# A mixture of experts that starts on the rows routed so far, while the last rows are still being routed

## The chip, the cores and the metric

The kernel runs on one core of a Trainium2 chip. A core has five engines that run side by side, each through its own instructions in order: TensorE (PE, matrix products; PEld is its loading of weights), VectorE (DVE), ScalarE (ACT), GpSimd (POOL) and SyncE (SP, which mostly issues DMAs). They wait for each other through semaphores. The metric is the device time of one execution in microseconds, and lower is better.

## The reference

A graph network of four layers over 2708 nodes with 256 features. Each layer is a graph part and a feed-forward part. The feed-forward part of the third layer (`_L2_ffn_ref`) is what the change touches: causal attention with four heads, and then a mixture of eight experts, of which each row uses its two best.

```python
x = x + y @ wo.T                                   # attention's result, added to the rows
flat = _rmsnorm(x, ln2_w).reshape(-1, Cx)
probs = jax.nn.softmax(flat @ router_w.T, axis=-1) # 8 experts
tp, ti = jax.lax.top_k(probs, TOPK)                # the best 2
tp = tp / (jnp.sum(tp, axis=-1, keepdims=True) + 1e-09)
weights = jnp.sum(tp[..., None] * jax.nn.one_hot(ti, NE, dtype=flat.dtype), axis=1)
for e in range(NE):
    hh = jax.nn.silu(flat @ w1[e].T) * (flat @ w3[e].T)
    out = out + weights[:, e:e + 1] * (hh @ w2[e].T)
return x + out.reshape(Bx, Tx, Cx)
```

Here `Bx*Tx` is the 2708 nodes. The experts' inner width is 682. The fourth layer's graph part (called g3 in the kernel) follows, and needs `W` and `a` of its own.

## The kernel before

**Attention** (`attention`) goes over the queries in six blocks: five of 512 columns and one of 148. Within a block, `attend` walks over the key tiles of 128 rows up to the diagonal. For each tile TensorE makes the scores (`sc`), ACT the exponential (`e`), DVE masks the diagonal, TensorE adds to the numerator (`po`), and the exponentials are summed for the denominator. These sums are kept in two parts: every third tile is added by GpSimd, the others by DVE. At the end of the block TensorE sums each part over its rows (`pd`), DVE takes the reciprocal and multiplies. The last block has both pairs of heads in one pass (m == 2) over 22 key tiles, the other blocks take one pair at a time.

**Routing** runs beside it. `send(n)` is a generator for the rows of one block: it multiplies with `wo` (`wy`), adds the result to `X`, normalises the row (`h`), makes the router's logits (`pr`), takes the first and second maximum, ranks the rows of each expert (`rank`), and scatters every row to two places of the DRAM tensor `hs` with indirect DMAs on GpSimd. In `hs` each expert has room for all rows, filled from the front. `between` moves the waiting generators on after each key tile, by a share of `steps[1]`. The rows of block n are sent during block n + 1. Those of the last block have no block after them: `send` for them runs alone, and then `finish` counts the rows of the experts and works out which expert each of 47 slot tiles of 128 rows belongs to. Slots 0 to 7 are always the first 128 rows of experts 0 to 7.

**The mixture** (`experts`) goes over the slot tiles with the function `through`. Per tile s: `fetch` loads the rows `f` from `hs` (on SP), `front` transposes them (`tp`, then a copy `ft` on ACT), `hidden` makes the two inner products `h0` (with `w1`) and `h1` (with `w3`), `silu` and `gate` combine them on ACT and DVE into `hh`, `transposes` transposes that on TensorE (`pt`) and copies it out (`ht`, partly on DVE and partly on ACT), `results` multiplies with `w2` (`po`), ACT copies to `y`, and GpSimd scatters `y` to the DRAM tensor `ys`. `place` (`where`) works out on DVE where these rows go in `ys`: to the node's row, or to a spare row where the slot is empty. It needs `own`, `taken` and `spare`, which `owners` makes after `finish`. In between stand `shares` (the softmax over the experts and the weights of the two choices) and, called from it, `Head`, which loads g3's `W` and `a` (`g3w`, `av`) through GpSimd's DMA queue and folds them on DVE. Tiles past the 47 are under a branch (`others`), for the case that the rows fall on the experts so unevenly that 47 don't suffice. The expert weights of one kind are 5.5 MB: `w1` comes in when the projections' room comes free, `w3` when attention's does.

The order of instructions on each engine is set at build time. `tc.issue_after` holds what stands under it behind a given instruction. Pools of buffers are opened and closed in the program's text, and what is opened in a closed pool's room waits for that room's last readers.

The lines touched: `decoder_ffn` (L1333), `Routing.finish` (L1528), `others` (L1596), `load` (L1613), `where` (L1633), `attention` (L1691) with `attend` and `send`, and `experts` (L1951).

Of the kernel before, what the change touches and what calls it, by code (L numbers as in the profile page):

```python
# [8 lines left out]
F32 = mybir.dt.float32  # L9
# [1323 lines left out]
def decoder_ffn(net, ctx):  # L1333

    nc, tc, a = net.nc, net.tc, net.a
    big = ctx.enter_context(tc.tile_pool(name="d_big", bufs=1))
    dram = ctx.enter_context(tc.tile_pool(name="d_dram", bufs=1, space=bass.MemoryType.DRAM))
    route = Routing(net, big, dram, 2, "d")  # L1340
    ln2 = net.load_rows(big, a["d_ln2"], D, "ln2")
    router = net.load_weight(big, a["d_routerT"], "router")
    with ExitStack() as inner:
        weights = Weights(net, inner)
        attention(net, route, ln2, router, weights)
        route.finish()
        prep = ctx.enter_context(tc.tile_pool(name="g3prep", bufs=1))
        work = inner.enter_context(tc.tile_pool(name="d_wt", bufs=1))
        heads = []

        def shares():

            route.weights(work)
            total = work.tile([P, NT], F32, name="total")
            nc.vector.tensor_tensor(total, route.weight[:, 0, :], route.weight[:, 1, :], ALU.add)
            nc.vector.tensor_scalar(total, total, 1e-9, None, ALU.add)
            nc.vector.reciprocal(total, total)
            for c in range(2):
                nc.vector.tensor_tensor(route.weight[:, c, :], route.weight[:, c, :], total, ALU.mult)
            heads.append(Head(net, prep, work, "g3", False))  # L1360

        experts(net, route, weights, shares)
    return heads[0], route
# [32 lines left out]
class Routing:  # L1396

# [6 lines left out]
    def __init__(self, net, pool, dram, choices, key):  # L1404
# [59 lines left out]
        nc.vector.memset(self.local[:, :E], 0.0)  # L1464
        self.total = pool.tile([P, E], F32, name=f"{key}total")
# [62 lines left out]
    def finish(self):  # L1528
# [4 lines left out]
        with tc.tile_pool(name=f"{self.key}finp", bufs=1, space=PSUM) as psum:  # L1533
            ps = psum.tile([P, E], F32, name="total")
            nc.tensor.matmul(ps, net.ones, self.count, start=True, stop=True)
            nc.vector.tensor_scalar(n, ps, 1.0, -1.0, ALU.max, ALU.add)
            nc.vector.tensor_copy(total, ps)
# [19 lines left out]
        nc.vector.tensor_copy(self.further, sums[:1, 3, 4 + E - 1 :])  # L1557

# [36 lines left out]
    @contextmanager  # L1595
    def others(self):  # L1596

        more = self.net.nc.values_load(self.further, min_val=0, max_val=self.tiles)
        with self.net.tc.If(more > self.usual - self.E):
            yield  # L1600
# [12 lines left out]
    def load(self, s, f):  # L1613

        sync = self.net.nc.sync
        if s < self.E:
            self.loaded = sync.dma_start(f, self.hs[s * CAP : s * CAP + P, :])
            return

        with nullcontext() if s == self.usual else self.net.tc.issue_after(self.loaded.ins):  # L1620
            row = sync.value_load(
                self.row[0:1, s : s + 1], min_val=0, max_val=(self.E - 1) * CAP + (NT - 1) * P
            )
        rows_of = self.hs[bass.ds(row, P), :]
        self.loaded = sync.dma_start(f, rows_of.rearrange("p d -> d p") if self.choices == 1 else rows_of)
# [7 lines left out]
    def where(self, work, s, f):  # L1633

        nc = self.net.nc
        to = work.tile([P, 1], I32, name="to", bufs=8)
        at = work.tile([P, 1], F32, name="second", bufs=3)
        nc.vector.tensor_scalar(  # L1638
            at, f[:, D + 1 :], self.own[:, s : s + 1], float(NT * P), ALU.not_equal, ALU.mult
        )  # L1640
        nc.vector.tensor_scalar(at, at, f[:, D : D + 1], self.taken[:, s : s + 1], ALU.add, ALU.mult)
        nc.vector.tensor_tensor(to, at, self.spare[:, s : s + 1], ALU.add)
        return to

    def send(self, to, y):
# [10 lines left out]
        tc.add_to_no_dep_group(f"{self.key}results", i.ins)  # L1656
        return i
# [33 lines left out]
def attention(net, route, ln2, router, weights):  # L1691
# [11 lines left out]
    with ExitStack() as ctx:  # L1703
        rp = ctx.enter_context(tc.tile_pool(name="a_r", bufs=2))
        one = ctx.enter_context(tc.tile_pool(name="a_one", bufs=1))
        psc = ctx.enter_context(tc.tile_pool(name="a_sc", bufs=2, space=PSUM))
        pso = ctx.enter_context(tc.tile_pool(name="a_o", bufs=2, space=PSUM))
        aux = ctx.enter_context(tc.tile_pool(name="a_x", bufs=2, space=PSUM))
# [12 lines left out]
        core = ctx.enter_context(ExitStack())  # L1721
# [71 lines left out]
        def attend(n, p):  # L1793
# [3 lines left out]
            if p == 0:  # L1797
                results[n] = rp.tile([P, 2, 512], F32, name="yt")
# [13 lines left out]
            for j in range(last + 1):  # L1812
# [7 lines left out]
                part = j % 3 == 2  # L1820
# [9 lines left out]
                nc.scalar.activation(ev, by_heads(ps[:r])[:, :, :, o:], AF.Exp, scale=DH**-0.5)  # L1830
# [22 lines left out]
            nc.vector.tensor_tensor(y, y, by_pairs(po), ALU.mult)  # L1853

        def send(n):
# [6 lines left out]
            for k, t in enumerate(its):  # L1862
                r = rows(t)
                po = aux.tile([P, D], F32, name="wy", tag="aux")
                net.matmul_k(po[:r], yt[:, :, k * P : k * P + r], wo)
                xa = xs[t] = rp.tile([P, D], F32, name="xa", bufs=4)
# [3 lines left out]
                h = hs[t] = rp.tile([P, D + 2], F32, name="h", bufs=8)  # L1870
# [9 lines left out]
            for k in range(0, len(its), 2):  # L1880
                pair = its[k : k + 2]
                ps = aux.tile([P, 2, 2 * P], F32, name="tp", tag="aux")
# [10 lines left out]
                pr = aux.tile([P, 2, 8], F32, name="pr", tag="aux")  # L1893
# [12 lines left out]
            yield from route.chunk(rp, aux, its[0], len(its), hs.__getitem__, tag="aux")  # L1906
# [18 lines left out]
        for n in range(len(cols)):  # L1925
# [4 lines left out]
            if n:  # L1930
                waiting.append(send(n - 1))
                steps[1] += 14
            for p in range(len(queries[n])):
                attend(n, p)
# [3 lines left out]
            waiting.clear()  # L1938
        core.close()
        weights.more()  # L1940
        for _ in send(len(cols) - 1):
            pass
# [8 lines left out]
def experts(net, route, weights, shares):  # L1951
# [4 lines left out]
    with ExitStack() as ctx:  # L1956
# [7 lines left out]
        def fetch(s):  # L1964
            fs[s] = work.tile([P, D + 2], F32, name="f", bufs=5)
            route.load(s, fs[s])
# [7 lines left out]
        def place(s):  # L1974
            tos[s] = route.where(work, s, fs.pop(s))
# [23 lines left out]
        def silu(s):  # L1999
# [3 lines left out]
            nc.scalar.activation(h2, halves.pop((s, 0))[:, :, :HALF], AF.Silu)  # L2003

        def gate(s):
            h2 = hhs[s][:, :HID].rearrange("p (q m) -> p q m", q=2)
            nc.vector.tensor_tensor(h2, h2, halves.pop((s, 1))[:, :, :HALF], ALU.mult)

        def transposes(s):
# [5 lines left out]
            nc.vector.tensor_copy(ht[:KP, :4, :], pt[:KP, 0])  # L2015
# [14 lines left out]
        def through(s0, s1):  # L2030


            for s in range(s0, min(s0 + 4, s1)):
                fetch(s)
# [5 lines left out]
            silu(s0)  # L2040
            front(s0 + 1)
# [3 lines left out]
            if s0 == 0:  # L2045
                route.owners()
            place(s0)
            place(s0 + 1)
            if s0 == 0:
                shares()  # L2050
            for s in range(s0, s1):
# [8 lines left out]
                silu(s + 1)  # L2060
                with tc.issue_after(last.ins):
                    last = results(s, ht)
                if s + 4 < s1:
                    fetch(s + 4)
                if s + 2 < s1:
                    with tc.issue_after(last.ins):
                        front(s + 2)
                        place(s + 2)
# [6 lines left out]
                gate(s + 1)  # L2075

        through(0, route.usual)
        with route.others():
            through(route.usual, route.tiles)
# [191 lines left out]
```

## Time and profile before

| | |
|---|---|
| time, median of 3 runs | 2853.9 us (2853.67 to 2859.36) |
| time of the profiled execution | 2853.26 us |
| its span | 2851.6 us |
| PE, DVE, ACT, POOL busy | 92%, 51%, 36%, 13% of the span |
| last attention block: first `po` to last `po` | 2056.05 to 2103.3 us |
| first transposes of the mixture | 2134.51 us |
| last `y` copied, last scatter issued | 2535.84, 2536.48 us |

The span is what the profiler saw from the first to the last instruction; the device time is about 1.7 us more. All places in time below are microseconds from the span's start. Busy time of TensorE is no measure of its speed, since matrix products overlap and the clock granted to it can be less than full; so the text goes by the waits and by the stretch concerned.

### The profile page before, as it was taken

How to read it: one execution, taken by the hardware profiler on the slowest of the kernel's cores; microseconds unless marked ns; L12 is line 12 of the kernel's file. 1: busy time of each engine (PE TensorE's matmuls, PEld its weight loads, DVE VectorE, ACT ScalarE, POOL GpSimd, SP SyncE). 2: the span in 40 equal slices, each digit the busy share in tenths (PEclk: the TensorE clock that was granted, in tenths of full speed). 3: DMA queues.
4: the chain of work that ended last, by engine and by line, in shares of the span. 5: the costliest groups of instructions: out<-in, count | busy, mean ns of one | idle time of the engine just before them, and what ended most of it. 6: DMA issues, size and time to landing. Idle time of an engine off the chain costs nothing.

```text
span 2851.6 us, 32365 instructions
## 1 busy us (share of the span) xinstructions
PE 2625.3 (92%) x11712; PEld 1616.6 (57%) x11712; DVE 1446.4 (51%) x3086; ACT 1040.0 (36%) x1639; POOL 381.5 (13%) x470
## 2 busy tenths in 40 slices
PE   5999989799999999888999899999969999969998
PEld 4667746563333444577788533333337777757885
DVE  7753348453777765422544456464653222245555
ACT  3344433224665653311543223233322221225453
POOL 1000012100000001143300123223331111110002
PEclk9999999797999999989999999899979999989999
DMA  8899210000000003753200100002031111041001
GB/s 295 288 299 326 97 65 1 3 5 1 1 1 1 1 3 115 169 176 128 85 1 1 34 23 18 16 0 94 16 117 32 30 30 34 28 137 62 1 1 40
DMA packets 107336, 197.67 MB, mean 69 GB/s; under 512 B 8831, under 2 KB 64361, under 8 KB 104341
## 3 DMA queue, kind: packets, MB, share of 16 engines
q1 hardware_dynamic: 89178, 147.89, 16.4%
q0 software_dynamic: 14624, 43.22, 4.6%
q10 hardware_dynamic: 3374, 4.46, 0.5%
q8 instruction: 98, 1.61, 0.2%
q14 instruction: 62, 0.50, 0.1%
HBM read 135.82 MB, written 59.71 MB: 69 GB/s over the span
## 4 chain that ended last, share of the span: by engine, by line
PE 74%; DVE 9%; issue 5%; DMA 5%; ACT 3%; POOL 3%; another core or an unknown queue 0%; ACTq 0%; SPq 0%; POOLq 0%; DVEq 0%
PE acc L1310 15%; PE acc L805 8%; PE acc L284 7%; PE den L816 4%; PE po L2022 4%; PE po L1836 3%; PE sc L1817 3%; PE score L273 3%; PE pv L123 3%; PE h L1990 3%; DMA f<-hs 2%; PE h L943 2%; PE po L123 2%; PE sc L1785 2%; PE pl L123 1%
## 5 line engine op out<-in xcount | busy, mean ns | idle before, releaser
L675 DVE SCALAR_TENSOR_TENSOR e<-e,mask 128x768 f32<-128x768 f32 (+2 forms) x264 | 411.3, 1573 | 310.2 <-ACT e L674 309.9
L674 ACT ACTIVATE e<-big_p,minus_one,ratio 128x768 f32<-128x768 f32 (+2 forms) x264 | 394.9, 1513 | 368.4 <-PE acc L1310 229.7
L1310 PE MATMUL acc<-V,e 128*128 128x257 f32 (+1 forms) x1936 | 433.5, 383 | 4.5 <-DVE e L675 4.4
L1310 PEld LDWEIGHTS acc<-V,e 128*128 128x128 f32 (+1 forms) x1936 | 352.3, 186 | 85.7 <-issue 32.1
L805 PE MATMUL acc<-e,V 128*64 128x512 f32 (+1 forms) x1056 | 244.3, 551 | 4.4 <-DVE e L675 4.4
L1990 PE MATMUL h<-w,ft 128*128 (+1 forms) x752 | 233.5, 453 | 0.5 <-ACT ft L1972 0.5
L284 PE MATMUL acc<-F,e 128*128 128x257 f32 x968 | 226.3, 384 | 3.1 <-DVE e L281 2.7
L284 PEld LDWEIGHTS acc<-F,e 128*128 128x128 f32 x968 | 173.4, 185 | 67.1 <-DVE e L281 28.5
L805 PEld LDWEIGHTS acc<-e,V 128*64 128x64 f32 x1056 | 107.5, 137 | 163.8 <-issue 131.2
L1817 PE MATMUL sc<-qt,kt 64*128 64x512 f32 (+5 forms) x568 | 177.2, 576 | 4.1 <-ACT e L1830 2.4
L1830 ACT ACTIVATE e<-sc 128x1024 f32<-128x1024 f32 (+3 forms) x120 | 99.6, 859 | 188.8 <-PE sc L1817 169.4
L1990 PEld LDWEIGHTS h<-w,ft 128*128 128x128 f32 x752 | 136.1, 191 | 56.7 <-issue 1.4
L281 DVE TENSOR_TENSOR e<-e,mask 128x512 f32<-128x512 f32 (+2 forms) x132 | 80.4, 625 | 150.3 <-ACT e L275 148.7
L1842 DVE TENSOR_TENSOR sum<-sum,e 128x1024 f32<-128x1024 f32 (+4 forms) x88 | 100.1, 1138 | 77.2 <-ACT e L1830 70.0
L275 ACT ACTIVATE e<-score 128x512 f32<-128x512 f32 (+2 forms) x132 | 69.7, 544 | 179.1 <-PE score L273 152.5
L2022 PE MATMUL po<-w,ht 114*128 (+1 forms) x564 | 129.5, 379 | 0.9 <-DVE ht L2015 0.9
L1836 PE MATMUL po<-e,V 128*64 128x512 f32 (+3 forms) x480 | 111.7, 547 | 16.8 <-ACT e L1830 8.7
L816 PE MATMUL den<-e,low 128*3 128x512 f32 (+1 forms) x1056 | 123.8, 542 | 0.3 <-DVE e L675 0.3
L2022 PEld LDWEIGHTS po<-w,ht 114*128 114x128 f32 x564 | 106.7, 189 | 22.6 <-DVE ht L2015 8.2
L1638 DVE TENSOR_SCALAR second<-f,down 128x1 f32<-128x1 f32 x47 | 9.9, 213 | 213.2 <-DMA f<-hs 213.2
L1817 PEld LDWEIGHTS sc<-qt,kt 64*128 64x128 f32 (+1 forms) x568 | 60.8, 191 | 94.1 <-issue 78.0
L273 PE MATMUL score<-QK 128*128 128x512 f32 (+2 forms) x264 | 112.1, 555 | 1.2 <-ACT e L275 0.7
(618 smaller groups left out, 3510.9 us busy)
## 6 DMA issues: line engine op xcount, KB each, us to landing
row<-in_adj SPq DMA_DIRECT2D x21, 1354.0 KB
raw<-in_adjT SPq DMA_DIRECT2D x35, 768.0 KB
hs<-zero SPq DMA_DIRECT2D x8, 2838.0 KB
hidden<-hr SPq DMA_DIRECT2D x34, 256.0 KB
wd<-in_f_wd SPq DMA_DIRECT2D x8, 1024.0 KB
kept<-mask SPq DMA_DIRECT2D x21, 338.5 KB
mask<-kept SPq DMA_DIRECT2D x21, 338.5 KB
f<-hs SPq DMA_DIRECT2D x47, 129.0 KB
```

What stands on the lines that cost most here:

```text
L123: self.nc.tensor.matmul(out, lhsT[:, c, :], rhs[:, c, :], start=first and c == 0, stop=last and c == n - 1)
L273: nc.tensor.matmul(ps[:r, :iw], QK[:, 0, span(j)], QK[:, 1, i0 : i0 + iw], start=True, stop=True)
L284: nc.tensor.matmul(acc[k][:ri], e[:r, k * P : k * P + ri], F[:r, j, :], start=j == 0, stop=j == NT - 1)
L674: nc.scalar.activation(v, big_p[:, i], AF.Relu, bias=net.minus_one, scale=ratio)
L675: return nc.vector.scalar_tensor_tensor(v, v, 1.0, net.mask[:, j, i], ALU.add, ALU.mult)
L805: made = nc.tensor.matmul(acc[n][half, :iw], V[:, j, h, :], e[:, k, i0 : i0 + iw], start=j == 0, stop=j == NT - 1)
L816: made = nc.tensor.matmul(den[g : g + Q, :iw], low[:, j, h, Q - 1 - q : 2 * Q - 1 - q], e[:, k, i0 : i0 + iw], start=False, stop=j == NT - ...
L1310: nc.tensor.matmul(acc[k][:ri], e[:, k * P : k * P + ri], V[:, j, :], start=j == 0, stop=j == NT - 1)
L1817: nc.tensor.matmul(by_pairs(ps[:r, g])[:, :, o:], kt[b, span(j)], qt[b, :, o:iw], start=True, stop=True)
L1836: nc.tensor.matmul(by_pairs(po[b])[:, :, o:], V[:r, j, g, :], by_pairs(e[:r, g])[:, :, o:], start=j == 0, stop=j == last,)
L1990: last = nc.tensor.matmul(halves[s, n][:, q, :HALF], fts[s][:, c, :], weights.w13[n][:, es[s], c, q * HALF : (q + 1) * HALF], start=c == 0 ...
L2022: last = nc.tensor.matmul(po, ht[:KP, k, :], w2[:KP, es[s], k, :], start=k == 0, stop=k == KC - 1)
```

## The change

Attention now ends by calling the mixture, with a generator for the rest of the routing, and the mixture runs that generator beside its first tiles.

- The rows of the fifth block are sent faster during the sixth: the count of steps for the last block is 24 instead of 14.
- In the last block all exponentials are summed on DVE, in one part; the result has a tile of its own, `yl`.
- `cut` counts the rows that each expert has had from the first five blocks (`so_many`), and makes `own`, `taken` and `spare` for slots 0 to 7 from that count.
- The first eight tiles are fetched at once, three on ACT's queue and five on GpSimd's, without waiting for the last block's rows, and are placed by the cut's counts. A row of the last block that would have come into one of these tiles is missing from it: `finish` counts these, and if there is any, the branch `others` runs all eight again.
- ACT loads Silu's table ahead of the first tile (`warm`).
- `routing()` is what runs beside the tiles: `send` of the last block, then `finish`, `owners` and `Head`, each one or more `step()`s. A step stands behind the last product of its place in the tile's work. `finish`, `owners` and `Head` are also held behind a given `ht` copy on DVE, and placing is held behind a gate.
- The tiles of the routing in PSUM share the one buffer of the mixture's `tp`.
- `shares` is taken apart from `Head` and stands at the end of the 47 tiles.

```diff
 def decoder_ffn(net, ctx):
+    prep = ctx.enter_context(tc.tile_pool(name="g3prep", bufs=1))
     with ExitStack() as inner:
         weights = Weights(net, inner)
-        attention(net, route, ln2, router, weights)
-        route.finish()
...
+        def head(work):
             heads.append(Head(net, prep, work, "g3", False))
 
-        experts(net, route, weights, shares)
+        def mixture(after, rest):
+            experts(net, route, weights, after, rest, head, shares)
+
+        attention(net, route, ln2, router, weights, mixture)
```

```diff
 class Routing:
+    def cut(self, psum, tag):
+        nc, E, pool, key = self.net.nc, self.E, self.pool, self.key
+        ps = psum.tile([P, E], F32, name="so_many", tag=tag)
+        nc.tensor.matmul(ps, self.net.ones, self.count, start=True, stop=True)
+        self.had = pool.tile([P, E], F32, name=f"{key}had")
+        nc.vector.tensor_scalar(self.had, ps, float(P), None, ALU.min)
+        own, taken, spare = self.cuts = [pool.tile([P, E], F32, name=f"{key}cut{k}") for k in range(3)]
+        nc.vector.tensor_scalar(own, self.part, self.at, None, ALU.add)
+        nc.vector.tensor_scalar(taken, self.had, self.at, None, ALU.is_gt)
+        nc.vector.tensor_tensor(spare, taken, self.place[:, :E], ALU.mult)
+        nc.vector.tensor_tensor(spare, self.place[:, :E], spare, ALU.subtract)
...
     def finish(self, psum=None, tag="total"):
...
+        if self.cuts:
+            missing = self.pool.tile([1, 1 + E], F32, name=f"{self.key}missing")
+            nc.vector.tensor_scalar(missing[:, 1:], total[:1], float(P), None, ALU.min)
+            nc.vector.tensor_tensor(missing[:, 1:], missing[:, 1:], self.had[:1], ALU.subtract)
+            nc.vector.tensor_reduce(missing[:, :1], missing[:, 1:], AX.X, ALU.add)
+            nc.vector.scalar_tensor_tensor(
+                self.further, missing[:, :1], float(S), sums[:1, 3, 4 + E - 1 :], ALU.mult, ALU.add
+            )
...
     def load(self, s, f, engine=None):
...
-            self.loaded = sync.dma_start(f, self.hs[s * CAP : s * CAP + P, :])
+            self.loaded = (engine or sync).dma_start(f, self.hs[s * CAP : s * CAP + P, :])
...
-    def where(self, work, s, f):
+    def where(self, work, s, f, cut=False):
+        own, taken, spare = self.cuts if cut else (self.own, self.taken, self.spare)
```

```diff
 def attention(...)
         def attend(n, p):
-                part = j % 3 == 2
+                part = j % 3 == 2 and m == 1
...
-        def send(n):
+        def send(n, rp, aux, tag="aux"):
...
-                steps[1] += 14
+                steps[1] += 14 if n + 1 < len(cols) else 24
...
+        route.cut(aux, "aux")
         core.close()
         weights.more()
-        for _ in send(len(cols) - 1):
-            pass
+        mixture(exp, lambda *work: send(len(cols) - 1, *work))
```

```diff
 def experts(...)
-        def through(s0, s1):
-            for s in range(s0, min(s0 + 4, s1)):
-                fetch(s)
+        def through(s0, s1, beside=iter(()), cut=False):
+            def step():
+                with tc.issue_after(last.ins):
+                    next(beside, None)
+
+            for s in range(s0, min(s0 + (E if cut else 4), s1)):
+                fetch(s, (nc.scalar if s < 3 else nc.gpsimd) if cut else None)
...
             silu(s0)
+            step()
             front(s0 + 1)
             for q in range(2):
                 last = hidden(s0, 1, q)
             gate(s0)
-            if s0 == 0:
-                route.owners()
-            place(s0)
-            place(s0 + 1)
-            if s0 == 0:
-                shares()
+            step()
+            with tc.issue_after(gates[-1].ins):
+                place(s0, cut)
+                place(s0 + 1, cut)
             for s in range(s0, s1):
...
                 silu(s + 1)
+                step()
                 with tc.issue_after(last.ins):
                     last = results(s, ht)
-                if s + 4 < s1:
+                step()
+                if s == 4:
+                    for _ in beside:
+                        pass
+                if s + 4 < s1 and (s + 4 >= E or not cut):
                     fetch(s + 4)
...
                 gate(s + 1)
+                step()
+                if s + 2 < s1:
+                    with tc.issue_after(gates[-1].ins):
+                        place(s + 2, cut and s + 2 < E)
...
+        def routing():
+            pool = ctx.enter_context(ExitStack())
+            yield from rest(pool.enter_context(tc.tile_pool(name="e_r", bufs=1)), pf, "tp")
+
+            with tc.issue_after(copied[-1].ins):
+                route.finish(pf, "tp")
+            yield
+            yield
+            with tc.issue_after(copied[-1].ins):
+                route.owners()
+            yield
+            pool.close()
+            room = ctx.enter_context(tc.tile_pool(name="e_room", bufs=1))
+
+            with tc.issue_after(copied[-1].ins), tc.issue_after(route.sent.ins):
+                head(room)
+            rooms.append(room)
+
+        with tc.issue_after(after.ins):
+            nc.scalar.activation(work.tile([P, 1], F32, name="warm", bufs=1), net.ln_eps, AF.Silu)
+        through(0, route.usual, routing(), True)
+
+        with tc.issue_after(silus[-1].ins), tc.issue_after(gates[-1].ins):
+            shares(rooms[0])
         with route.others():
+            through(0, E)
             through(route.usual, route.tiles)
```

Here `after` is the last exponential of attention, `copied`, `gates` and `silus` are lists of the instructions put out so far, and `route.sent` is the last scatter of a tile's result.

## The prediction

> **What bounds the kernel now.** I read the page first (span 2851.6 us, PE busy 92%), then the chain of waits in the stretch that the change touches, then TensorE's timeline there, then the windows for the granted clock. The mixture (`experts`, 47 tiles) is TensorE work end to end: from 2149.88 us every tile is the same chain.
>
> ```profile
> 2107.83 1.28 PE pd L1848 x4
> ...
> 2133.73 4.60 DMA av<-in_g_a
> ...
> 2149.88 3.44 PE h L1990 x12
> 2153.32 0.75 PE pt L2014 x6
> 2154.07 1.15 PE h L1990 x4
> 2155.22 2.59 PE po L2022 x12
> 2157.81 0.22 PE tp L116 x2
> ```
>
> Columns are start, duration, what. A tile costs 3.44+0.75+1.15+2.59+0.22 = 8.15 us of TensorE and nothing else. Ahead of that lies a hole. TensorE's timeline (brackets: idle before, and who ended it):
>
> ```profile
> 2107.83 1.25 PE L1848 MATMUL pd<-sum,ones 128*64 128x296 f32 x4 [3.77 <-POOL sum L1842]
> 2111.68 3.90 PE L123 MATMUL wy<-wo,yt 128*128 128x256 f32 x8 [2.60 <-DVE yt L1853]
> ...
> 2134.51 0.66 PE L116 MATMUL tp<-ident,f 128*128 128x128 f32 x2 [9.30 <-POOL hh L2001]
> 2135.64 4.78 PE L1990 MATMUL h<-w,ft 128*128 128x341 f32 x8 [0.46 <-ACT ft L1972]
> ```
>
> Attention's last `po` ends at 2103.34. Then TensorE waits for GpSimd's partial sum, for DVE's reciprocal, and for the routing of the last two row tiles, until the first mixture tile starts at 2134.5. From 2103.34 to the second gate's matmuls at 2149.88 are 46.5 us, for 11.7 us of mixture work at full speed.
>
> ```profile
> 2105.00:2106.00 1.00, 0.00 (x0) 0.00 (x0) 0.00 (x0) 0.00 (x0) 0.69 (x2) 1.00 0.37 132
> 2106.00:2107.00 1.00, 0.00 (x0) 0.00 (x0) 0.00 (x0) 0.00 (x0) 0.97 (x2) 0.51 0.16 58
> ...
> 2139.00:2140.00 1.00, 1.00 (x3) 0.56 (x2) 1.00 (x5) 0.00 (x0) 0.00 (x0) 0.50 0.00 0
> 2140.00:2141.00 1.00, 1.00 (x5) 0.61 (x5) 1.00 (x6) 0.55 (x1) 0.00 (x0) 0.92 0.00 0
> ```
>
> The third number from the end is the granted clock: it falls to a half about 2.0 us after TensorE stops (2104.0), and is back 5.6 us after it works again (2134.5). A stall costs twice.
>
> ```profile
> 2132.37 17.86 SPq L1617 DMA_DIRECT2D f<-hs  x8
> ...
> 2135.60 1.28 ACT L2003 ACT_TABLE_LOAD   x1
> ```
>
> The first rows `f` were read by TensorE 2.1 us after their issue; a table load on ACT takes 1.28 us.
>
> [...] the trace shows 1.28 and an ACTIVATE straight behind it at 2538.43, so I take 1.28.
>
> **The change, step by step.** Times are on the profiled run's axis (run 2853.26, span 2851.6; the median shown is 2853.9, so sums carry over within 0.6 us).
>
> S1, last attention block. The third of the sums that GpSimd did (7 adds of 1.45 us) goes to DVE (0.78 each, 5.5 us in all); `send` of the block before is squeezed from all 22 key tiles into about the first 13 (24 steps instead of 14). DVE was busy about 29 of 50 us there. In the squeezed part I count reciprocal and product 4.0, adds 10.1, `send` 15.7 = 29.8 us of DVE against 36 us of TensorE, so DVE is tight but not the bound: 0 to 3 us lost, I take 1. Gain: the scatters of that block end by about 2099 instead of 2111.5, and `pd` no longer queues behind GpSimd's scatters. With one more add (0.8) `pd` ends at 2104.4, not 2109.08.
>
> S2, first rows. ACT loads Silu's table once the last `po` and the scatters are done: 2103.4+1.28 = 2104.75, then issues three `f` loads (0.43 each on SP); +2.1 = 2106.85. The `w3` load (8 x 682 KB) starts at the same moment, because it still waits for `pd`. From nothing to 2 us on top; I take 0.75: 2107.6. `w3`'s first expert is needed only about 2114, and 682 KB at the 400 GB/s of windows 2114 to 2126 take 1.7 us, so it hides. The other five `f` go through GpSimd (about 0.8 us an issue), needed tiles later.
>
> S3, first tile. TensorE has stood for 3 us, so half clock: transposes 0.66, copy 0.46, 8 x 0.57 = 4.6, to 2113.3. Full clock after that: `wy` of 128 rows 0.86, `h` with `w3` 2.3, next transposes 0.22, `wy` of 20 rows 0.86: 2117.6. Then `h` 2.3, `pt` 0.75, `po` 2.59, `tp` 0.22 and 0.5 for an `ht` copy that stands behind two placings and the start of the inverse root on DVE: 2124.0. This is the place that was 2149.88. **Gain 25.9.** DVE's reciprocal (2.0) and product (0.46) now lie beside `f`'s latency.
>
> S4, routing beside tiles 1 to 3. TensorE still does it: transposes 0.5, `pr` 1.06, `rank` 0.8, `total` 0.4 = 2.8 us, now at full clock. **Loss 2.8.** On DVE the first-max chain (about 5 us) fits between an `ht` copy (0.69) and the gate (0.87) of a tile. `finish` does not quite: `rank`'s followers 2 us, then about 14 ops of 0.2 and 3 of 0.47 before gate 3. That gate comes about 1.8 us late, and the `ht` copy behind it, with one 0.47 reduce and five small ops between, 0.7 more. **Loss 2.3** (0 to 5). `owners` (3.4 us) fits in the next tile.
>
> S5, `Head` (g3's folded weights). Its two DMAs are issued on GpSimd behind the scatter of tile 3, and DVE reaches its first op behind gate 4 and a placing. Tile 3's `po` ends about 2153.35; y copy 0.4, scatter 1.3, `g3w` 0.8, so `av` is issued at 2155.9. Landing: 4.7 us in this trace (2133.73 to 2138.43, beside eight `f` loads), 2.9 for the similar load at 572.0 (DVE read it at 574.9). I take 3.0: 2158.9. Eight ops, about 3.0, then the `ht` copy 0.69: 2162.6. TensorE wants that copy after `h` and `pt` of the next tile, 2158.95. **Loss 3.7** (0 to 6), and TensorE has stood long enough for half clock: 3.7 us at half cost 1.9. **Loss 1.9** (0 to 2.8). Queued behind DVE's wait are this copy, ACT's copy of the other chunks, `po` 4, and through it everything.
>
> S6, things without price. `hs` scatters of the last block stand on GpSimd before tile 2's `y` scatter (4 x 1.28): three `y` buffers give it two tiles, 16 us. The SP load of tile 8 waits for these scatters and `row`, ready about 2155, needed near 2180. `shares` moves to the end: 15 DVE ops, about 4 us, and an Exp with a table load; the weight is first used at 2545.29, 9 us after the last `y` copy (2535.84), and three of the ops stand before the last `ht` copy in what was a 0.96 us idle. At most 0.1; without that cover about 4. The branch for experts short at the cut never runs: in the reference, the first 2560 rows give each expert at least 485.
>
> Sum: 25.9 - 2.8 - 2.3 - 3.7 - 1.9 - 1 (S1) = **14.2 us**: 2853.26 - 14.2 = **2839**.
>
> **Rivals.**
> A, better: `av` lands early or the clock stays up, so S5 costs little and S4 hides: gain 18 to 24, 2829 to 2835. For: first-tile work is all dependency-free by then. Against: in this trace DVE waited for `av` both times a `Head` was built (12.6 us in three waits with the first graph's).
> B, worse: DVE is the bound in the last block (S1's 3) and in tiles 1 to 4 (S4 5, S5 6+2.8) and `f` comes 2 us later: 25.9-2-2.8-5-8.8-3 = gain 4, 2844 to 2851. For: DVE's order is fixed, so one late input holds gates and copies. Against: DVE was busy 25.6 of 40 us even in the hole.
> C, slower: the half clock stays. Bursts at 2107.83 (1.25 us) and 2111.68 (3.9 us) left it at 0.50. If gaps of over 2 us recur in tiles 0 to 4, their 41 us of TensorE work run at half: 41 us more, of which my sum holds 4.7 and the stalls 6 lie inside: gain 14 turns into a loss of 10 or more, about 2864. It decides once the half clock lasts 30 us longer than I count. Against: my gaps are one at the start and one in tile 4, with about 50 us between.
>
> **Numbers.** Forecast case (gain 9 to 18, 2835 to 2844) 0.60; A 0.17; B 0.15; C 0.07; nothing measurable 0.01. Half of B's upper end lies within 0.2% (5.7 us, what a measurement of this kernel can tell). Faster 0.87, same 0.06, slower 0.07. The range takes the forecast case, most of A and most of B: 2831 to 2848.
>
> **What would show it.** S1 and S2: `pd` near 2104, `f` read near 2107. S3: the second gate's first matmul near 2124. S4: a gate some 2 us late in tile 3. S5: DVE waiting for `av` with `po` of tile 4 some 4 us late, and one dip of the clock. S6: first use of the weight unchanged after the last `y`. It is wrong if `f` comes after 2111, if DVE runs behind from the last block on, or if the clock stays at a half past tile 0.

## The result

The changed kernel took **2825.6 us** (median of 4 runs, 2823.7 to 2828.0) beside 2854.3 for the kernel before (4 runs, 2853.7 to 2859.4): ratio 0.9891, 95% interval 0.9876 to 0.9906. That is 28.7 us less, twice the 14.2 that I forecast, and outside my range. The profiled execution took 2823.73 us, its span is 2822.0.

A line of the page of the changed kernel:

```profile
L2046 DVE TENSOR_TENSOR hh<-hh,h 128x682 f32<-128x682 f32 x47 | 40.7, 865 | 247.5 <-PE h L2029 247.5
```

This is DVE's gate (busy us and mean ns, then idle us before it and what ended that): DVE's idle time in the mixture (247.5 us) now ends with TensorE's products. The page before has no such row among its costliest; that idle time stood in another row:

```profile
L1638 DVE TENSOR_SCALAR second<-f,down 128x1 f32<-128x1 f32 x47 | 9.9, 213 | 213.2 <-DMA f<-hs 213.2
```

There DVE waited 213.2 us for the loads of the tiles' rows. The gate itself needs TensorE's products and no load: where DVE stood waiting for a load, something else stood in front of the gate in its queue.

TensorE around the start of the mixture, changed kernel (start, duration, what, in brackets idle before and who ended it):

```profile
2103.60 0.72 PE L1870 MATMUL po<-e,V 128*64 128x296 f32 x4 [1.46 <-DVE e L1868]
...
2107.22 0.66 PE L116 MATMUL tp<-ident,f 128*128 128x128 f32 x2 [1.43 <-DMA f<-hs]
2108.39 4.60 PE L2029 MATMUL h<-w,ft 128*128 128x341 f32 x8 [0.52 <-ACT ft L2011]
...
2123.24 2.17 PE L2029 MATMUL h<-w,ft 128*128 128x341 f32 x7
```

The first transposes come at 2107.22 where they came at 2134.51, and the second gate's first product at 2123.24 where I forecast 2124.0. So the part that I worked out at length looks right to 0.8 us. That is partly luck: counted from the last attention block's first result `po`, which came 3.1 us later in this execution (below), the place is 3.9 us earlier than forecast. Where is the rest? The gates, one for each of the 47 tiles, mark the mixture's pace, so I cut the span at the first results of the last attention block (its first `po`), at gates 0, 7 and 46, and at the end. Microseconds, from the start times of these instructions in the profiles:

| kernel | first `po` to gate 0 | to gate 7 | to gate 46 | to the end | sum |
|---|---|---|---|---|---|
| before | 88.1 | 57.4 | 328.8 | 321.3 | 795.6 |
| changed | 57.3 | 67.1 | 317.9 | 320.5 | 762.9 |
| difference | -30.8 | +9.8 | -10.9 | -0.8 | -32.7 |

The changed kernel's profiled execution reached the first `po` 3.1 us later (2059.14, not 2056.05). In other executions below this place lies anywhere from 2049.1 to 2059.7, though no edit touches what lies before it; I don't count it. The last column but one also moves by 3 us among kernels that are the same there.

So the first two stretches gained 21.0 us together, and **10.9 us came in 39 tiles of the steady mixture**, which my sum didn't touch. In the kernel before, the gates came 8.15 us apart up to the seventh, then 8.49 us (34 intervals, 2193.06 to 2481.65), then 8.15 again for the last ones. In the changed kernel they are 8.155 apart from gate 5 to gate 45. The chain of waits of the kernel before says why, in a stretch that I hadn't looked at:

```profile
2198.84 2.00 DMA f<-hs
...
2200.87 0.23 DVE second L1638
...
2201.51 0.88 DVE hh L2007
...
2207.04 0.23 PE tp L116 x2
...
2207.29 2.07 DMA f<-hs
```

The products `h` that the gate reads are not what it waits for. The chain goes: transposes `tp` of a tile, then the load of rows `f`, then DVE's three placing operations (`second`, `second`, `to`), then the gate `hh`, then TensorE. A placing of some tile stands before the gate in DVE's queue, its rows are loaded only when `tp` has freed a buffer, and the gate waits behind. The same DVE stretch in the changed kernel:

```profile
2305.94 0.87 DVE L2046 TENSOR_TENSOR hh<-hh,h 128x682 f32<-128x682 f32 x1 [5.64 <-PE h L2029]
2306.72 0.21 DVE L1668 TENSOR_SCALAR second<-f,down 128x1 f32<-128x1 f32 x1
```

Here the gate comes first and waits for TensorE alone, and the placing follows.

In the source both kernels place tile s+2 at about gate s+1. But the source order isn't the order of DVE's queue. In the built kernel before, nothing ties the placing to the gate, and the scheduler moved it up as far as the buffers let it: ahead of gate k the queue holds the placing of tile k+**6**. With five `f` buffers, the rows of tile k+6 go into the buffer of tile k+1, and TensorE transposes that one just before gate k. And what stands ahead of the gate there holds it, as the traces show: in the changed kernel a gate starts 2.79 us after the transposes before it (2303.15 and 2305.94), here 3.08 us after (2198.43 and 2201.51), right behind `to`, which started at 2201.43. The gate stood about 0.3 us behind work that it doesn't need. Up to the seventh gate only the first of the three operations stood ahead of it and the gate was not late; from the eighth on, all three did.

### The profile page after: what moved, and what is told of

It is laid out like the page before. It is cut to its first block, busy times and chain, and to the rows that moved or that the text cites. A ratio compares the mean times of both kernels' runs of the same rounds, so it can differ in the third digit from the quotient of the medians.

```text
span 2822.0 us, 32381 instructions
## 1 busy us (share of the span) xinstructions
PE 2612.0 (93%) x11710; PEld 1613.5 (57%) x11710; DVE 1451.8 (51%) x3102; ACT 1041.2 (37%) x1641; POOL 375.3 (13%) x469
## 4 chain that ended last, share of the span: by engine, by line
PE 77%; DVE 7%; issue 5%; DMA 4%; ACT 3%; POOL 2%; SPq 0%; ACTq 0%; POOLq 0%; DVEq 0%
PE acc L1310 15%; PE acc L805 8%; PE acc L284 7%; PE h L2029 7%; PE den L816 4%; PE po L2061 4%; PE po L1870 4%; PE sc L1850 3%; PE score L273 3%; PE pv L123 3%; PE h L943 2%; PE sc L1816 2%; PE po L123 2%; DMA dys<-y,to 2%; PE pl L123 1%
## 5 line engine op out<-in xcount | busy, mean ns | idle before, releaser
L1864 ACT ACTIVATE e<-sc 128x1024 f32<-128x1024 f32 (+4 forms) x121 | 100.2, 857 | 186.4 <-PE sc L1850 170.1
L2046 DVE TENSOR_TENSOR hh<-hh,h 128x682 f32<-128x682 f32 x47 | 40.7, 865 | 247.5 <-PE h L2029 247.5
L1876 DVE TENSOR_TENSOR sum<-sum,e 128x1024 f32<-128x1024 f32 (+5 forms) x95 | 104.7, 1102 | 77.4 <-ACT e L1864 74.2
L1870 PE MATMUL po<-e,V 128*64 128x512 f32 (+4 forms) x484 | 113.2, 546 | 17.2 <-DVE e L1868 9.0
```

The source lines that it names most:

```text
L1870: nc.tensor.matmul(by_pairs(po[b])[:, :, o:], V[:r, j, g, :], by_pairs(e[:r, g])[:, :, o:], start=j == 0, stop=j == last,)
```

## The experiments

Three theories of the 10.9 us. **1, order:** the placing ahead of the gate costs it, and the change's hold (`issue_after(gates[-1].ins)`) took it away. **2, late rows:** five `f` buffers are too few, and the change's eight cured it. **3:** the gain comes from the end of the mixture or the last graph layer. The first two experiments change the kernel before, the others the changed one.

### Only the hold, in the kernel before

```diff
                     with tc.issue_after(last.ins):
                         front(s + 2)
-                        place(s + 2)
...
                 gate(s + 1)
+                if s + 2 < s1:
+                    with tc.issue_after(gates[-1].ins):
+                        place(s + 2)
```

> The kernel before, with one thing of the change: DVE's placing of a tile's rows is held until the gate of the tile before it has been issued. Theory 1 (in the kernel before, each gate from the eighth tile on stands on DVE behind a placing of a tile six ahead, whose rows have only just been loaded; gates came 8.49 us apart, 34 times, for 8.155 of TensorE work): the gates come 8.15 to 8.16 us apart throughout, 34 x 0.333 = 11.3 us less, 2843.0 (2841 to 2845). Theory 2 (the rows come late because five buffers hold them, and the change's eight cure that): five buffers stay, so no gain, 2854. Theory 3 (the extra 12 us come from the end of the mixture or from the last graph layer): no gain here, 2854.

Measured: 2842.2 us (9 runs) beside 2855.5 for the kernel before (45 runs), ratio 0.9963 (0.9947 to 0.9978). The gates come 8.15 or 8.16 us apart throughout, and gate 7 to gate 46 takes 317.9 us, as in the changed kernel. On DVE the gate at 2299.28 now waits 5.64 us for TensorE's `h`, and the placing follows it, as in the changed kernel.

A moved call of one function, with five buffers as before, takes the whole 10.9 us. Theories 2 and 3 fall as causes of the gain.

### Only the eight buffers, in the kernel before

```diff
-            fs[s] = work.tile([P, D + 2], F32, name="f", bufs=5)
+            fs[s] = work.tile([P, D + 2], F32, name="f", bufs=E)
```

> The kernel before, with eight buffers for the tiles' rows instead of five and nothing else. Theory 1 (order on DVE): its placings only run further ahead, until the ring is full again, and stand before the gates as now: no gain, within 2 us of the kernel before, gates still 8.4 to 8.5 us apart. Theory 2 (late rows): the rows are there long before they are placed, DVE waits for none, and the gates come 8.16 us apart: 2843. Theory 3: 2854.

Measured: 2867.0 us (22 runs), ratio 1.0045 (1.0033 to 1.0058): slower, which none of the theories had said. The gates are mostly 8.74 us apart, with single ones of 9.0, 9.5 and 10.1. DVE at one of the worst:

```profile
2291.77 0.21 DVE L1638 TENSOR_SCALAR second<-f,down 128x1 f32<-128x1 f32 x1 [5.46 <-DMA f<-hs]
...
2293.82 0.16 DVE L1642 TENSOR_TENSOR to<-second,dspare 128x1 int32<-128x1 f32 x1 [1.53 <-DMA dys<-y,to]
2293.90 0.86 DVE L2007 TENSOR_TENSOR hh<-hh,h 128x682 f32<-128x682 f32 x1
```

With three more buffers the first of the three placing operations ran nine tiles ahead, not six, and again stood before a gate. The last one, `to`, ran only seven ahead: it has eight buffers of its own, so it waits for the scatter (`dys`) of the tile just before the gate's, 0.15 to 0.4 us as a rule and 1.53 us here. This second ring now sets the pace. In the chain of waits from 2210 to 2480 us the loads `f` take 0.8% of the time and `dys` takes 27.3%; in the kernel before the loads take 24.2% there and `dys` is not among the parts listed. So the eight buffers did take the late rows out of the chain, and another wait in front of the same gate took their place. Theory 1 had forecast no gain and a time within 2 us of the kernel before; it didn't have the second ring, and the 11.5 us of loss are a miss. Whether more buffers for `to` as well would have helped was not tried.

### The changed kernel without the hold

```diff
                 if s + 2 < s1:
-                    with tc.issue_after(gates[-1].ins):
+                    with tc.issue_after(last.ins):
                         place(s + 2, cut and s + 2 < E)
```

> The changed kernel without that hold: the placing of a tile is free to stand ahead of the gate, all else as changed (eight buffers for the rows, first tiles beside the routing). Theory 1: from about the eighth tile on the gates are 8.45 to 8.5 us apart again, 30 to 35 times 0.33 = 10 to 11.5 us more than the changed kernel, 2836 to 2837; more if the first tiles' gates too come to stand behind rows that are loaded late (to 2842). Theories 2 and 3: as the changed kernel, 2825.6 within 2.

Measured: 2849.3 us (21 runs), ratio to the kernel before 0.9971 (0.9959 to 0.9984). Gate 7 to gate 46 takes 338.3 us instead of 317.9, gates 8.73 us apart. This is the second experiment's pace, and it had to be: the changed kernel has eight buffers. I had expected the five buffers' 8.49, and a loss of 10 to 16 us beside the changed kernel, where it is about 23. Without the hold, four fifths of the change's gain would be gone.

### The folded weights two tiles later

The stall that I forecast for tile 4 is there. All engines of the changed kernel, a few rows:

```profile
2152.39 0.60 POOL L86 DMA_DIRECT2D av<-in_g_a  x1
...
2156.71 0.43 DVE L657 TENSOR_TENSOR a1t<-g3w,av 128x256 f32<-128x256 f32 x1 [2.63 <-DMA av<-in_g_a]
...
2159.36 0.68 DVE L2054 COPY ht<-pt 114x512 f32<-114x512 f32 x1
...
2160.10 4.54 PE L2061 MATMUL po<-w,ht 114*128 114x256 f32 x12 [4.58 <-DVE ht L2054]
```

DVE waits for `av`, the copy `ht` stands behind its eight operations, and TensorE stands for 4.58 us; then the results take 4.54 us instead of 2.75, at half clock (0.50 granted from 2161 to 2163). The edit leaves the two loads and moves the operations, half of them behind the copy of tile 5 and half behind that of tile 6:

```diff
-                head(room)
+                head[0](room)
             rooms.append(room)
+            for c in range(2):
+                for _ in range(6 if c == 0 else 3):
+                    yield
+                with tc.issue_after(copied[-1].ins):
+                    head[1](room, c)
```

> The changed kernel with the two loads of the last layer's folded weights issued where they are now, but DVE's eight operations on them two and three tiles later, half behind one copy and half behind the next. If the hole in tile 4 is DVE standing before a load that takes 4.3 us (4.6 us of stall, and 1.8 of the next results at half clock), it goes: 6.4 us less than the changed kernel, 2819.2 (2818 to 2821); the operations, 1.5 us a tile, lie in the 5.6 us that DVE has idle in each. If the hole is only moved (the load later still, or the operations delay a copy by their length), 2822 to 2826.

Measured: 2818.1 us (5 runs), ratio to the kernel before 0.9865 (0.9842 to 0.9889). Gate 4 to gate 5 takes 8.16 us instead of 14.68, and DVE has room for the operations between a copy and the next gate:

```profile
2162.86 0.69 DVE L2062 COPY ht<-pt 114x512 f32<-114x512 f32 x1 [0.33 <-PE pt L2061]
2163.47 0.41 DVE L657 TENSOR_TENSOR a1t<-g3w,av 128x256 f32<-128x256 f32 x1
...
2169.19 0.86 DVE L2054 TENSOR_TENSOR hh<-hh,h 128x682 f32<-128x682 f32 x1 [3.94 <-PE h L2037]
```

The stall was the wait and nothing else: 6.5 us, all of it gone.

### The last attention block: its two parts, alone and together

The changed kernel again, for comparison on one chip with the next two:

> The changed kernel once more, for its times beside the three others on the same chip. All theories: about 28.7 us less than the kernel before (ratio 0.989 to 0.991); gates 8.155 us apart from the sixth on; tile 4's results again about 4.6 us late.

Measured: 2827.8 us (6 runs), ratio 0.9907 (0.9889 to 0.9925); the first gate 57.4 us after the block's first `po`.

GpSimd keeps its third of the sums:

```diff
-                part = j % 3 == 2 and m == 1
+                part = j % 3 == 2
```

> The changed kernel with GpSimd keeping its third of the sums in the last attention block (seven adds of 1.45 us), all else as changed. If DVE's taking them is what lets that block end earlier (from the block's first po to the end of pd: 53.0 us before, about 46.4 in the changed kernel): pd waits for GpSimd's sum again, its end 3 to 6 us later, the first tile as much, 2829 to 2832 beside 2825.6. If the early end comes from the quicker routing of the block before (its scatters out of GpSimd's way by 2102): GpSimd's adds are late by no more than 1 us, 2825 to 2827.

The old pace of the routing:

```diff
-                steps[1] += 14 if n + 1 < len(cols) else 24
+                steps[1] += 14
```

> The changed kernel with the routing of the block before spread over the last block as it was (14 steps instead of 24). If the quick pace matters for the first rows: that block's last scatters land only when the block ends or after it, the first rows are loaded 2 to 6 us later, the first tile starts as much later, 2828 to 2832. If the pace matters little: within 1 us of the changed kernel, with DVE less crowded early in the block.

Both of these edits at once:

> The changed kernel with both parts of the last attention block undone: GpSimd keeps its third of the sums and the routing of the block before is spread in 14 steps. If the two parts only work together (the quick routing puts eight scatters of 1.28 us in a row on GpSimd, and GpSimd's adds would stand behind them; without it the scatters end after the block): this is no worse than the version with 14 steps alone plus the pd wait, 2842 to 2848, the first gate 75 to 80 us after the block's first results (88.1 before, 57.3 changed, 75.0 with 14 steps alone). If they add up as independent gains (10 us and 17.7 us at the first gate): about 85 us, 2850 to 2855.

And the first once more, since its profile and its times said different things:

> The version in which GpSimd keeps its third of the last block's sums, once more, since its profiled execution was 11 us behind the changed kernel's (GpSimd's adds behind eight scatters, exponentials waiting 4.6 us for their buffer, the clock at a half) and its other runs only 1 to 2. If that stall comes in every execution: 2833 to 2838 (the changed kernel 2827.8 on that chip). If it comes in some: 2826 to 2834, and its profile without the stall has the first gate 57 to 60 us after the block's first results, not 67.

| last block | first `po` to gate 0 | median, us | ratio to before |
|---|---|---|---|
| as changed | 57.3 and 57.4 | 2827.8 | 0.9907 (0.9889 to 0.9925) |
| GpSimd's third | 67.4 and 67.4 | 2830.0 and 2831.1 | 0.9912 (0.9895 to 0.9928), 0.9913 (0.9889 to 0.9936) |
| 14 steps | 75.0 | 2842.2 | 0.9959 (0.9943 to 0.9975) |
| both | 77.4 | 2845.5 | 0.9957 (0.9940 to 0.9974) |

The quick pace is the larger part: 17.7 us at the first gate with the sums on DVE, where I had expected 2 to 6 at most. In the kernel with 14 steps, TensorE is done with the block 1.4 us later, counted from its first `po`, and then:

```profile
2108.54 0.97 POOL L1524 DMA_INDIRECT hs<-h,dto  x1 [0.30 <-issue]
...
2115.40 1.31 ACTq L1646 DMA_DIRECT2D f<-hs  x3
...
2121.64 0.66 PE L116 MATMUL tp<-ident,f 128*128 128x128 f32 x2 [18.27 <-DMA f<-hs]
```

The last scatter is issued at 2108.54, the rows can be read only at 2115.4, and TensorE gets them 6.2 us after their issue, having stood for 18.27 us. In the changed kernel the same load is read 2.27 us after its issue (2104.95 to 2107.22). What differs is the place of the 5.5 MB of `w3`: its issues began at 2103.19 here, and at 2105.61 there, after those of `f`. On SP the eight issues take 18.69 us here and 8.05 us there. No run moved `w3` alone; that it holds up the scatters and the rows is read from the traces and not tested.

With GpSimd's third kept, the parts get in each other's way, as I had not foreseen. All engines of the repeated run:

```profile
2095.62 0.97 POOL L1524 DMA_INDIRECT hs<-h,dto  x1 [0.30 <-issue]
2096.61 1.44 POOL L1876 TENSOR_TENSOR sum<-sum,e 128x592 f32<-128x592 f32 x1
2098.08 0.66 ACT L1864 ACTIVATE e<-sc 128x592 f32<-128x592 f32 x1 [4.59 <-POOL sum L1876]
...
2098.80 1.26 PE L1870 MATMUL po<-e,V 128*64 128x296 f32 x4 [3.84 <-ACT e L1864]
```

The quick routing puts its eight scatters in one row on GpSimd, an addition stands behind them, the exponential waits for its buffer, and TensorE stands for 3.84 us; its four products behind the wait then take 1.26 us, where four like them took 0.72 before it. Both profiles of this kernel show it, 10 us at the first gate. Its other runs don't show it clearly: the medians are 2 to 3 us above the changed kernel's, and the ratios 0.9912 and 0.9913 lie beside 0.9907. Whether the stall is shorter in executions without a profile stays open. The order of size does not: the pace matters more than where the sums are made.

The row with both parts undone holds one more thing. There the mixture's first tiles still run ahead of the last routing, and the first gate comes 10.7 us sooner than in the kernel before (77.4 beside 88.1), but the next seven tiles take 9.8 us more, with the routing and the wait for `av` among them. **Running the first tiles early, with the block as it was, gained 0.9 us** in these two profiles. The 21.0 us of the changed kernel need the rows to be there when the block ends. The opposite case, the quick pace and DVE's sums without the early start, was not run.

### TensorE's clock at the first tile

The first tile's eight products took 4.60 us in the changed kernel, at half clock (the third number from the end of each line, here the first and the last microsecond with a part of it, 0.50 in all those between):

```profile
2105.00:2106.00 1.00, 0.79 (x6) 0.30 (x2) 1.00 (x3) 1.00 (x1) 0.60 (x3) 0.85 0.05 5
...
2112.00:2113.00 1.00, 1.00 (x4) 0.67 (x3) 0.00 (x0) 0.00 (x0) 0.00 (x0) 0.73 1.01 378
```

So the half clock lasted from about 2105.7 to 2112.5. I tried to keep the clock up with products that nothing uses (a 128x512 product of `ones` with `wo`), on top of the version with the later folding. First three of them behind the last `pd`:

> The version with the folded weights' operations two tiles later, plus three matmuls of 128x512 that nothing uses, between the last pd and the count of the rows routed so far; they stand on TensorE in the time in which the first rows are loaded (2105.8 to 2107.5 there). If the half clock of the first tile (its eight matmuls 4.63 us) comes from that idle time, the clock stays up, the eight take about 2.4, and the whole is 2 us less than that version. If the 1.5 us of idle before it (2102.6 to 2104.0, the wait for the last exponentials and their mask) already brings the clock down, the eight stay at 4.6, the filling itself runs at half clock and delays the first transposes: 0 to 2 us more.

Measured: 2816.7 us (4 runs), ratio 0.9867 (0.9847 to 0.9886), no different from the version without them (0.9865). TensorE (each of the products shows as two instructions):

```profile
2101.68 0.72 PE L1881 MATMUL po<-e,V 128*64 128x296 f32 x4 [1.46 <-DVE e L1879]
...
2103.47 4.54 PE L1548 MATMUL fill<-wo,ones 128*128 128x512 f32 x6
...
2108.92 2.56 PE L2040 MATMUL h<-w,ft 128*128 128x341 f32 x8 [0.52 <-ACT ft L2022]
```

and its clock:

```profile
2103.00:2104.00 1.00, 1.00 (x5) 0.32 (x4) 1.00 (x4) 1.00 (x1) 0.52 (x3) 0.91 0.02 1
...
2107.00:2108.00 1.00, 1.00 (x5) 0.43 (x4) 0.00 (x0) 0.00 (x0) 0.00 (x0) 0.89 0.97 341
```

The clock fell to a half at about 2103.8 (0.91 of that microsecond, 0.50 in the next three) though TensorE had been at work since 2101.68, and came back at about 2107.2 in the middle of the filling, which therefore took 4.54 us and delayed the first tile by about as much as that tile then saved. So the idle time behind `pd` did not bring the clock down. It has a part all the same: with it filled the half clock lasted 3.4 us instead of 6.8, and the first tile ran at full clock (2.56 us). What lay before the fall was a wait of 1.46 us for the last exponentials and their mask. I put one product into that wait and one behind `pd`:

```diff
+                if m == 2 and j == last:
+                    fill = aux.tile([P, 512], F32, name="fill", tag="aux")
+                    nc.tensor.matmul(fill, net.ones, wo.rearrange("p c d -> p (c d)"), start=True, stop=True)
```

> The version with the folded weights' operations later, plus two unused matmuls of 128x512, one in TensorE's wait for the last exponentials and their mask (1.46 us), one after the last pd. If the half clock of the first tile comes from that first wait (with three of them behind pd alone the clock fell all the same, while they ran): now it stays up, the eight matmuls of the first tile take 2.3 to 2.6 us instead of 4.63, and the first gate comes 2 us earlier, 55.3 us after the block's first results instead of 57.1. If any idle time behind pd brings it down by itself: 4.6 again, and the first gate at 57 or later.

Measured: **2812.0 us** (5 runs) beside 2857.0 for the kernel before, ratio 0.9847 (0.9824 to 0.9871). TensorE and a slice of its clock:

```profile
2098.53 1.13 PE L1865 MATMUL fill<-wo,ones 128*128 128x512 f32 x2
2100.07 0.72 PE L1883 MATMUL po<-e,V 128*64 128x296 f32 x4 [0.40 <-DVE e L1881]
...
2104.59 2.53 PE L2042 MATMUL h<-w,ft 128*128 128x341 f32 x8 [0.60 <-DMA f<-hs]
```

```profile
2102.00:2103.00 1.00, 0.99 (x2) 0.16 (x2) 1.00 (x2) 0.84 (x2) 1.00 (x2) 1.00 0.49 137
2103.00:2104.00 1.00, 0.80 (x4) 0.50 (x4) 1.00 (x2) 0.00 (x0) 1.00 (x3) 1.00 0.88 204
2104.00:2105.00 1.00, 0.41 (x2) 0.35 (x3) 0.93 (x6) 0.37 (x1) 0.73 (x2) 1.00 0.96 360
```

The clock stays at 1.00 (from 2094 to 2112), the eight products take 2.53 us, and the first gate comes 55.0 us after the block's first `po`, 2.1 sooner than without filling (57.1). From the first `po` to the end this version takes 754.7 us, the changed kernel 762.9 and 765.7 in its two profiles. It has the lowest median of all versions here, but its interval overlaps those of the two versions with the later folding (0.9865 and 0.9867): that the filling gains 2 us is read from the profile, and the times can't confirm so little. Whether the product in the wait would do alone was not tried.

The traces show when the clock fell and came back, not what decides it. In the changed kernel and in the version with three products behind `pd` it fell 2.1 us after work had begun again (2103.60 and 2105.7, 2101.68 and 2103.8), and it was back after 6.8 and 3.4 us. In the kernel before, TensorE works again from 2054.53, at the start of the last block, having stood for 2.35 us; the clock falls at about 2054.8 and is back at about 2058.2. So it fell in all three while TensorE was at work. In these versions the filling that kept it up lay where the idle time was, not where the slow products were. That the product in the wait did it, and not some other difference of the last version's one profile, is my reading and was not shown.

## Why the prediction was wrong

The direction was right, the mechanism of the first part too; the sum was 14 us short. Taken by its steps, from the block's first `po`:

- **The step that failed** is the first one: "from 2149.88 us every tile is the same chain", and "a tile costs 3.44+0.75+1.15+2.59+0.22 = 8.15 us of TensorE and nothing else". I read this from one tile at the start, and gave it to all 47. From the eighth gate to the 41st they cost 8.49 us. So the held placing, which stands in the diff in two lines, has no term in my sum; it is worth 10.9 us, shown by making that edit alone. The page held the sign, 213.2 us of DVE waiting for `f`, and the prediction passes over it. In the first seven tiles that wait cost nothing; from the eighth to the 41st it held the gate.
- **S1**, the last block: 1 us of loss forecast. In fact its last `po` ends 45.7 us after its first, where it was 47.4: a gain of 1.7. Term wrong by 2.7 us, in size and sign. For the quicker pace of `send` I had a place, "by about 2099", and no price; it is what the first tiles stand on, 17.7 us.
- **S2**, the first rows: read at 2107.6 forecast, 2107.22 measured; on the block's clock 51.6 and 48.1 us. Besides S1's 1.7 us, two terms were too dear: the table load (1.28) didn't delay the DMA issues of ACT's queue, which went out 0.06 us after it had started; and `f` beside `w3` took 2.27 us, not 2.85, of which 0.75 was an estimate that no stretch of the trace before showed.
- **S3**, the first tile at half clock: 4.6 us forecast and measured. Its cause I had as the time for which TensorE stands before `f`. By the fillings, as I read them, it was the wait before the last `po`: with three products behind `pd` alone the clock fell all the same, with one in that wait too it stayed at 1.00. The time before `f` only kept it down for the first tile (6.8 us at a half, 3.4 with that time filled).
- **S4**, routing beside tiles 1 to 3: 2.8 and 2.3 us forecast. From gate 1 to gate 4 the changed kernel takes 26.8 us where three tiles cost 24.5: 2.3 us in all. TensorE waits 0.2 us for gate 3, so `finish` is nearly hidden; the 2.3 for it is the term that was too large.
- **S5**, the folded weights: 3.7 and 1.9 us forecast; gate 4 to gate 5 takes 6.5 us more than a tile. DVE had `av` 4.3 us after its issue, not the 3.0 that I took; the issue itself came 2.4 us after tile 3's results, about as forecast (2.55), and the eight operations took 2.65 us, not 3.0. Place, order and cause are as forecast.
- **S6**: nothing forecast. From the last gate to the end the changed kernel takes 320.5 us, the kernel before 321.3, so `shares` at the end costs nothing that shows.

In numbers: 14.2 forecast, +2.7 (S1), +1.8 (S2), +0.4 (S3), +2.8 (S4), -0.9 (S5) is the 21.0 us up to gate 7. The held placing adds 10.9, and the last stretch 0.8; the block's later start takes 3.1 of these 32.7 back in the profiled execution. Rival A (better) had the right size for the first part, 18 to 24 us, but with the stall of S5 gone, which it wasn't. Rivals B and C did not come: from tile 0 to tile 4, TensorE waited for DVE only 0.2 us at gate 3 and 4.58 us in tile 4, where DVE waited for `av`; and the clock fell to 0.50 once at the start and once in tile 4.

## What to carry to other kernels

Read a long loop in its steady state, not only at its edge: measure the distance between two of its landmarks over the whole length before calling it a constant, and open the chain of waits where the distance changes. Look at where the scheduler puts work that nothing ties to its place: here it moved the placing ahead on DVE until that waited for the end of a buffer ring, and the gate behind it waited too (8.49 us from gate to gate instead of 8.155); a tie was the cure, and three more buffers in one ring made it worse (8.74). And price the arrival of the first inputs before the work that is to be overlapped: here the early start gained 0.9 us with the last block as it was, and 21.0 with the rows there when the block ended.

## What the runs showed of the hardware

- The DMA issues on ACT's queue went out 0.06 us after a table load of 1.28 us had begun on ACT (2104.95 and 2104.89), not behind it.
- A load of 128 rows was read by TensorE 2.27 us after its issue (2104.95 to 2107.22) when the 5.5 MB of `w3` were issued behind it, from 2105.61, and 6.2 us after (2115.40 to 2121.64) when they had been issued from 2103.19 on, 12 us ahead.
- In that second case, the one with 14 steps, eight scatters were issued 1.27 to 1.37 us apart on GpSimd from 2099.52 to 2108.54, and the wait for them ended at 2115.33.
- In the version with three products behind `pd`, TensorE's clock fell to a half 2.1 us after a wait of 1.46 us had ended (2101.68 and 2103.8), with TensorE at work all that time but for 0.19 us. With products in the wait (0.40 us of it left) and behind `pd`, the clock stayed at 1.00.
